# Seven block products for the Down projection of a pair in an attention and mixture-of-experts block

## The chip, the cores and the metric

The kernel runs on one core of a Trainium2 chip. The metric is the device time of one execution in microseconds. All arithmetic that matters here is fp32.

## The reference

One layer over 4096 tokens of 256 features. The input is normalised to `xn`, and three terms are added: the input, a windowed attention block with its own dense MLP, and a mixture of eight experts of which each token uses two.

```
xn = layernorm(x)
out = x + attn_block(xn) + experts(xn)

attn_block: q, k, v = xn@Wq+bq, ...;  window 64, 8 heads, softmax over a band
            y = layernorm(xn + o@Wo + bo)*gamma + beta
            y + gelu(y@W1 + b1)@W2 + b2           # 256 -> 1024 -> 256
experts:    top 2 of 8 by softmax(xn@gate_w.T + gate_b), shares made to sum to 1
            for each expert e (hidden size 816):
              h = silu((xn@gp_w[e].T + gp_b[e]) * (xn@up_w[e].T + up_b[e]))
              acc += share[:, e] * (h @ down_w[e].T + down_b[e])
```

## The kernel before

Tokens are sorted by expert into units. A unit is a pair of tiles (256 tokens) or a single tile (128 tokens) of one expert. 34 units are always worked through, in the list `UNITS`: 30 pairs, and singles at places 3, 7, 11 and 15. Five more at the end (`MAYBE`) run under a condition, by the function `whole`.

A unit needs three things: the gathered rows turned into `xT` (`gather`, `turned`), the hidden chunks, and Down. The hidden size 816 is 6 chunks of 128 (`FCM`) and a rest of 48 (`REM`). `glu` computes one chunk: gate and up matmuls into one PSUM bank `gu`, ScalarE adds the gate's bias (`gs`, L853), VectorE multiplies into `hT` (L854). The rest of a pair lies in one more chunk of `hT`: tile 0's on partitions 0 to 47, tile 1's on 64 to 111. `silu` runs on `hT` in place. Down (`results_rest` L896, `results` L907) takes the hidden tile as the stationary operand and the expert's weights `wd`, 256 columns wide, as the moving one, into one bank per tile (`pe`); `summed` (L917) adds the bias, which `wd` carries on all partitions, into `y`, and a DMA stores `y` to the table `done`. An fp32 matmul leaves two records in the trace.

The loop runs over steps b = 0 to 33. Step b computes the hidden chunks of unit b and the Down of unit b - 1. In the first 32 steps (`STEPS`) it also does one half (four heads, `hq` = b % 2) of the attention of two query tiles:

- `scores`: PE writes four banks `ps` (L960); VectorE adds the mask and takes the maximum into `pr` (L974); `exps` on ScalarE (L989)
- `merge`, four times, on GpSimd: two operations on `pr` (L1001, L1002). `apart`, on GpSimd: differences of neighbouring values into `xd` (L1009)
- `scale`, on VectorE: the reciprocal `rec` (L1019), then `pr` times `rec` (L1021), the sums of the second half (L1022, L1023), and on GpSimd `xd` times these (L1025)
- `flip`: PE transposes `pr` into a bank `pT` (L1030), VectorE masks it twice into `prT` (L1034). `flip_rest`: PE's two small transposes of `xd` into `pX` (L1043)
- `weigh`, `outputs`, and in each even step from the second on `closing` for the two tiles before (L1074, L1077, and their moments)

The order on every engine is written out by hand: `tc.manual_schedule` keeps the order of the code. Within a step it is: gathers, scores, `apart`, Down of the rest, chunk 0, chunk 1, `closing`, `scale`, Down, the load of `wd`, `turned`, projections for later tiles (steps 1 to 16), chunk 2, `flip`, chunk 3, `flip`, `flip_rest`, chunk 4, the rest, chunk 5, `weigh`. In steps 32 and 33 there is no attention and Down follows chunk 0. Behind the loop comes the Down of unit 33. The PSUM pool has seven banks; a new tile takes the one whose last use stands earliest in the order.

Behind the units the second part runs: the dense MLP. There `second` (L1198) already computes its product with W2 by seven block products in place of eight, with sums made by `sums_of_weights` and `sums_of_hidden`.

Of the kernel before, what the change touches and what calls it, by code (L numbers as in the profile page):

```python
# [32 lines left out]
F32 = mybir.dt.float32  # L33
# [8 lines left out]
P = 128  # L42
S = 4096
D = 256
# [10 lines left out]

REM = FE % P
REM_UP = P // 2
FM = FE - REM  # L60
FCM = FM // P
NT = S // P
G = 512
NG = S // G
# [24 lines left out]

GW, UW, RW, BW = 0, DC * FM, 2 * DC * FM, 2 * DC * FM + DC * P  # L90
GU = BW + 2 * FCM + 1
DN = FCE * D + D
HQ = 4
AHEAD = 4
WARM = 50
# [6 lines left out]
def block_kernel(ctx: ExitStack, tc: tile.TileContext, a: dict, out: bass.AP):  # L102
# [116 lines left out]

    att = ctx.enter_context(ExitStack())  # L220
    wqkv = pool(att, "wqkv", right)
    mask = wqkv.tile([P, 4, 2 * P], F32, tag="mask", name="mask")

# [87 lines left out]
    def make_mask():  # L311

        nc.gpsimd.memset(mask, 0.0)
        for kind in range(4):

            def keep(base, step, channel, m=mask[:, kind, :]):
                nc.gpsimd.affine_select(
                    out=m,  # L320
                    in_=m,
                    compare_op=ALU.is_ge,
                    fill=MASKED,
                    base=base,
                    pattern=[[step, 2 * P]],
                    channel_multiplier=channel,
                )

            keep(0, 1, -1)
            keep(2 * WIN, -1, 1)  # L330
            if kind == 0:
                keep(-WIN, 1, 0)
            if kind == 3:
# [551 lines left out]
    def silu(hT, lo, hi, on=slice(0, P)):  # L885
        nc.scalar.activation(hT[on, lo:hi, :], hT[on, lo:hi, :], AF.Silu)  # L886

    def silu_rest(hT):

        silu(hT, FCM, FCE, slice(0, REM_UP + REM if hT.shape[2] > P else REM))  # L890

    def results_rest(pds, w, hT):
        for t, pd in enumerate(pds):

            half = slice(t * REM_UP, (t + 1) * REM_UP) if len(pds) > 1 else slice(0, P)
            nc.tensor.matmul(  # L896
                pd,
                hT[half, FCM, t * P : (t + 1) * P],
                w[half, FCM * D : FCE * D],
                start=True,  # L900
                stop=False,
            )
# [9 lines left out]
                    stop=(f == FCM - 1),  # L912
                )

    def summed(y, pds, w):
        for t, pd in enumerate(pds):
            nc.vector.tensor_tensor(y[:, t, :], pd, w[:, FCE * D :], ALU.add)  # L917

    def down_rest(b, w, hT):

# [1 line left out]
        results_rest(pds, w, hT)  # L922
        return pds

    def down(b, pds, w, hT):
        at, n, _ = UNITS[b]
        results(pds, w, hT)
        y = he.tile([P, TB, D], F32, tag="y", name=f"y{b}")[:, 0:n, :]
        summed(y, pds, w)
        nc.sync.dma_start(out=rows(done, at, n), in_=y)  # L930

    def whole(b, w, wd, xT, hT, banks, gss, y):

        _, n, _ = UNITS[b]
        n_in = n * P
        for k, f in enumerate([FCM] + list(range(FCM))):
            pb = halves(banks[k % 3])[:, :, 0:n_in]
            gs = gss[k % 3][:, 0:n_in]
            if f == FCM:
                rest_of(w, xT, hT, pb, gs)  # L940
            else:
# [8 lines left out]
        summed(y, pds, wd)  # L950

    def scores(i, hq):

        g = i // TG
        ps = [halves(bank(f"ps{i}_{hq}_{hh}")) for hh in range(HQ)]
        for j in range(2):
            lo = (i + j) % TG * P
            for hh in range(HQ):
                r = slice(hh * DH, (hh + 1) * DH)
                nc.tensor.matmul(  # L960
                    ps[hh][:, j, :],
                    qts[g][r, hq, lo : lo + P],
                    kts[g][r, hq, lo : lo + 2 * P],
                    start=True,
                    stop=True,
                )
        kind = 0 if i == 0 else 2 if i == NT - 2 else 1
        pr = sp.tile([P, HQ, 2, 2 * P], F32, tag="pr", name=f"pr{i}_{hq}", bufs=1)

        nm = sp.tile([P, 2, HQ], F32, tag="nm", name=f"nm{i}_{hq}")  # L970
        sums = sp.tile([P, 2, HQ], F32, tag="sums", name=f"sums{i}_{hq}")
        for hh in range(HQ):
            for j in range(2):
                nc.vector.tensor_tensor_reduce(  # L974
                    out=pr[:, hh, j, :],
                    in0=ps[hh][:, j, :],
                    in1=mask[:, kind + j, :],
                    scale=-1.0,
                    scalar=-LOWEST,
                    op0=ALU.add,  # L980
                    op1=ALU.min,
                    accum_out=nm[:, j, hh : hh + 1],
                )
        return pr, nm, sums
# [26 lines left out]
            )  # L1011
        return xd

    def scale(i, hq, pr, sums, xd):

        rec = sp.tile([P, 2, HQ], F32, tag="rec", name=f"rec{i}_{hq}")
        same = sp.tile([P, 2, HQ], F32, tag="same", name=f"same{i}_{hq}")
        by_head = "p j h -> p h j"
        nc.vector.reciprocal(rec, sums)  # L1019
        first = pr[:, :, :, 0:P]  # L1020
        nc.vector.tensor_tensor(first, first, bcast(rec.rearrange(by_head), P, 3), ALU.mult)  # L1021
        nc.vector.tensor_reduce(same.rearrange(by_head), pr[:, :, :, P:], AX.X, ALU.add)  # L1022
        nc.vector.tensor_tensor(same, same, rec, ALU.mult)  # L1023
        xh = xd.rearrange("p j (h d) -> p j h d", h=HQ)
        nc.gpsimd.tensor_tensor(xh, xh, bcast(same, DH, 3), ALU.mult)  # L1025

    def flip(i, hq, j, pr):
        pb = bank(f"pT{i}_{hq}_{j}")
        for hh in range(HQ):
            nc.tensor.transpose(pb[:, hh * P : (hh + 1) * P], pr[:, hh, j, 0:P], ident)  # L1030

        prT = [sp.tile([P, HQ, P], F32, tag="prT", name=f"prT{i}_{hq}_{j}"), pr[:, :, j, P:]]
        for t, m in zip(prT, (first_keys, second_keys)):
            nc.vector.tensor_tensor(  # L1034
                t, pb.rearrange("p (h q) -> p h q", h=HQ), bcast(m, HQ, 1), ALU.mult
            )
        return prT
# [204 lines left out]
    hTs = [he.tile([P, FCE, B], F32, tag=f"hT{k}", name=f"hT{k}", bufs=1) for k in range(2)]  # L1242
    for k in range(2):
        nc.gpsimd.memset(hTs[k][:, FCM, :], 0.0)
    res = {0: residual(0)}
    xT = {}
    pos, oTs = {}, {}
# [11 lines left out]
    for b in range(ALWAYS):  # L1259
# [5 lines left out]
        def chunk(f):  # L1265
            glu(b, f, gus[b], xT[b], hT)

        if b + 2 < ALWAYS:
            xs[b + 2] = gather(b + 2)
        if attends:  # L1270
            pr, nm, sums = scores(i, hq)
            xd = apart(i, hq)
        if 0 < b < STEPS:
            pds = down_rest(b - 1, downs[b - 1], hTs[(b - 1) % 2])
        if b == 0:
            xT[0] = turned(0, xs.pop(0))
        if attends:
            exps(pr, nm, sums, 0, 3)
            merge(pr, 0)
        chunk(0)  # L1280
        if b >= STEPS:
            pds = down_rest(b - 1, downs[b - 1], hTs[(b - 1) % 2])
            down(b - 1, pds, downs.pop(b - 1), hTs[(b - 1) % 2])
        if attends:
            exps(pr, nm, sums, 3, 6)
            merge(pr, 1)
# [5 lines left out]
        if hq == 0 and i - 2 in res:  # L1292
            closing(i - 2, oTs.pop(i - 2), res.pop(i - 2))
            if i < STEPS:
                res[i] = residual(i)
        if attends:
            scale(i, hq, pr, sums, xd)
        if b == STEPS:
            att.close()
            wf = pool(ctx, "wf", right)  # L1300
# [14 lines left out]
        if b == STEPS + 1:  # L1315
# [2 lines left out]
            nc.vector.scalar_tensor_tensor(shift2, mv2[:, :, 0], -1.0, r2, ALU.mult, ALU.mult)  # L1318
            nc.vector.tensor_tensor(beta_b2, beta, b2, ALU.add)
            x2s[0] = second_loads(0)  # L1320
        if 0 < b < STEPS:
            down(b - 1, pds, downs.pop(b - 1), hTs[(b - 1) % 2])
        if b == ALWAYS - 1:
            load_unit(ALWAYS + 1)
        if b + 1 < ALWAYS:
# [28 lines left out]
        if attends:  # L1354

            if b == 0:
                prT0 = flip(i, hq, 0, pr)
                chunk(4)
            prT1 = flip(i, hq, 1, pr)
            added = flip_rest(i, hq, xd)  # L1360
        if b:
            chunk(4)
        n = b - (ALWAYS - len(MAYBE))
        if n >= 0:
            flags[ALWAYS + n] = nc.values_load(used[0:1, n : n + 1], min_val=0, max_val=1)
# [18 lines left out]
    down(ALWAYS - 1, pds, downs.pop(ALWAYS - 1), last)  # L1384
    load_unit(ALWAYS + 2)
    for b in range(ALWAYS, BLOCKS):
        at, n, _ = UNITS[b]
# [139 lines left out]
```

## Time and profile before

| | |
|---|---|
| runs | 1085.88, 1086.16, 1087.51 us, median 1086.16 |
| profiled execution | 1082.57 us, span 1080.4 us |
| TensorE clock granted | 1.00 |
| busy: TensorE, VectorE, ScalarE, GpSimd | 1069.1, 657.6, 526.9, 452.0 us |
| the loop's 32 attention steps | 82 to 797 us, about 22 us each |
| conditional units | 822 to 859 us |
| the dense MLP | 859 us to the end |

Busy time of the engines, in tenths, stands in the page in 40 slices. A line of a group has the source line, the engine, the operation, what is written and read, its shape, how often it ran, the busy time, the mean duration of one in ns, and the idle time ahead of it with what ended that. A line of a timeline has the start from the beginning of the span, the duration, the engine, the operation, and in brackets the idle time before it and what ended it.

### The profile page before, as it was taken

The numbers are of one execution on the slowest core, as the hardware profiler recorded it, in microseconds if no ns is written. First come the engines' busy times: TensorE is split into PE (matmuls) and PEld (weight loads), VectorE is DVE, ScalarE is ACT, GpSimd is POOL, SyncE is SP. The second block draws the span as 40 slices with busy tenths as digits, with TensorE's granted clock in tenths as the row PEclk, the third lists the DMA queues.
The fourth block names the chain that finished last, engine by engine and source line by source line (L and its number), as shares of the span: only waits on it lengthen the run. The fifth ranks groups of instructions, "written<-read, shape, count | busy, mean of one in ns | idle before, by whom it ended". The sixth has DMA issues, their size and how long they took to land. (4 is left out here: it accounts for less than half of the span.)

```text
span 1080.4 us, 19051 instructions
## 1 busy us (share of the span) xinstructions
PE 1069.1 (99%) x6802; PEld 857.4 (79%) x6802; DVE 657.6 (61%) x1709; ACT 526.9 (49%) x1225; POOL 452.0 (42%) x599
## 2 busy tenths in 40 slices
PE   9999999999999999999999999999999999999998
PEld 6577888887888788888888888888888847777778
DVE  6666666657666566666666766666533355555546
ACT  4527446554556545745564566555424363333320
POOL 5525544455445454554445534544520043222220
PEclk9999999999999999999999999999999999999999
DMA  8252445544445354544544545445575443333121
GB/s 274 84 221 92 142 137 177 177 151 154 160 142 187 132 164 159 202 142 159 171 180 142 181 149 199 142 139 184 177 242 223 160 141 111 97 96 97 59 64 40
DMA packets 61040, 163.42 MB, mean 151 GB/s; under 512 B 6576, under 2 KB 46896, under 8 KB 51472
## 3 DMA queue, kind: packets, MB, share of 16 engines
q1 hardware_dynamic: 53216, 143.92, 38.0%
q0 software_dynamic: 6480, 17.70, 6.2%
q8 instruction: 55, 0.90, 0.3%
q10 hardware_dynamic: 1248, 0.56, 0.2%
q14 instruction: 41, 0.34, 0.1%
HBM read 140.28 MB, written 21.89 MB: 150 GB/s over the span
## 5 line engine op out<-in xcount | busy, mean ns | idle before, releaser
L845 PE MATMUL gu<-xsT,wg 128*128 128x256 f32 (+1 forms) x1632 | 362.5, 369 | 0.7 <-ACT xsT L837 0.7
L845 PEld LDWEIGHTS gu<-xsT,wg 128*128 128x128 f32 x1632 | 289.1, 190 | 45.3 <-DVE nm L974 8.6
L853 ACT ACTIVATE gs<-gu,wg 128x256 f32<-128x256 f32 (+1 forms) x204 | 92.6, 454 | 255.8 <-PE gu L845 244.1
L854 DVE SCALAR_TENSOR_TENSOR hT<-gu,wg,gs 128x256 f32<-128x256 f32 (+1 forms) x204 | 95.0, 467 | 174.7 <-ACT gs L853 174.5
L1001 POOL TENSOR_TENSOR pr<-pr 128x256 f32<-128x256 f32 x128 | 93.2, 728 | 250.6 <-ACT pr L989 250.6
L907 PE MATMUL pe<-wd,hT 128*128 128x256 f32 x768 | 171.6, 379 | 0.0
L907 PEld LDWEIGHTS pe<-wd,hT 128*128 128x128 f32 x768 | 145.4, 190 | 20.5 <-issue 1.0
L1172 POOL DMA_INDIRECT got<-done,slot x64 | 64.4, 1007 | 176.6 <-DVE acc L1185 110.7
L1002 POOL TENSOR_TENSOR pr<-pr,ident 128x256 f32<-128x256 f32 x128 | 125.4, 979 | 10.0
L989 ACT ACTIVATE pr<-pr,nm 128x256 f32<-128x256 f32 x256 | 126.7, 497 | 0.4
L1127 PE MATMUL ph<-x2T,W 128*128 128x512 f32 x256 | 111.4, 593 | 1.1 <-ACT x2T L1117 1.1
L974 DVE CUSTOM_DVE_ANT_0 pr<-ps,mask 128x256 f32<-128x256 f32 x256 | 90.7, 420 | 22.8 <-PE ps L960 22.8
L1134 ACT ACTIVATE hf<-ph,b 128x512 f32<-128x512 f32 x64 | 43.4, 688 | 118.4 <-issue 54.6
L886 ACT ACTIVATE hT<-hT 128x512 f32<-128x512 f32 (+3 forms) x148 | 80.9, 546 | 32.0 <-DVE hT L854 22.4
L1127 PEld LDWEIGHTS ph<-x2T,W 128*128 128x128 f32 x256 | 48.0, 190 | 58.9 <-issue 53.6
L819 POOL DMA_INDIRECT xs<-xnd,token x71 | 68.8, 969 | 48.6 <-DVE paired_tiles L786 31.3
L1021 DVE TENSOR_TENSOR pr<-pr,rec 128x1024 f32<-128x1024 f32 x32 | 39.6, 1236 | 27.9 <-POOL pr L1001 27.9
L1208 DVE TENSOR_TENSOR acc<-u,acc 128x256 f32<-128x256 f32 x32 | 12.9, 422 | 70.2 <-ACT u L1211 69.6
L989 ACT ACT_TABLE_LOAD x31 | 39.8, 1283 | 23.7 <-DVE nm L974 23.6
L1022 DVE TENSOR_REDUCE same<-pr 128x8 f32<-128x1024 f32 x32 | 39.1, 1221 | 19.2 <-POOL pr L1002 19.2
L989 ACT ACTIVATION_READ_ACCUMULATOR pr<-pr,nm 128x1 f32 x256 | 48.3, 189 | 0.0
L1198 PE MATMUL s<-V,hv 128*128 128x128 f32 x384 | 44.2, 275 | 0.0
(231 smaller groups left out, 1573.3 us busy)
## 6 DMA issues: line engine op xcount, KB each, us to landing
wg<-in_gate_up SPq DMA_DIRECT2D x37, 1670.5 KB, 7.0
wd<-in_down SPq DMA_DIRECT2D x37, 1024.0 KB, 5.5
done<-y SPq DMA_DIRECT2D x30, 256.0 KB, 2.2
x<-in_x SPq DMA_DIRECT2D x8, 512.0 KB, 5.5
xnd<-xn SPq DMA_DIRECT2D x8, 512.0 KB, 4.3
res<-xnd SPq DMA_DIRECT2D x16, 256.0 KB, 2.9
x1d<-res SPq DMA_DIRECT2D x16, 256.0 KB, 2.2
x<-x1d SPq DMA_DIRECT2D x8, 512.0 KB, 4.7
```

The source lines that it names most:

```text
L819: nc.gpsimd.indirect_dma_start(out=x[:, t, :], out_offset=None, in_=xnd, in_offset=bass.IndirectOffsetOnAxis(ap=token[:, i : i + 1], axis=0),)
L845: nc.tensor.matmul(pb[:, k, :], w[:, lo : lo + P], xT[:, c, :], start=(c == 0), stop=(c == DC - 1),)
L853: nc.scalar.activation(gs, pb[:, 0, :], AF.Identity, bias=w[:, gb : gb + 1])
L854: nc.vector.scalar_tensor_tensor(hT[:, f, :], pb[:, 1, :], w[:, ub : ub + 1], gs, ALU.add, ALU.mult)
L886: nc.scalar.activation(hT[on, lo:hi, :], hT[on, lo:hi, :], AF.Silu)
L907: nc.tensor.matmul(pd, hT[:, f, t * P : (t + 1) * P], w[:, f * D : (f + 1) * D], start=False, stop=(f == FCM - 1),)
L974: nc.vector.tensor_tensor_reduce(out=pr[:, hh, j, :], in0=ps[hh][:, j, :], in1=mask[:, kind + j, :], scale=-1.0, scalar=-LOWEST, op0=ALU.a ...
L989: nc.scalar.activation(pr[:, hh, j, :], pr[:, hh, j, :], AF.Exp, bias=nm[:, j, hh : hh + 1], scale=-1.0, accum_out=sums[:, j, hh : hh + 1],)
L1001: nc.gpsimd.tensor_tensor(first, first, second, ALU.add)
L1002: nc.gpsimd.tensor_tensor(second, second, bcast(ident, 2, 1), ALU.mult)
L1127: nc.tensor.matmul(ph, W1[:, c, f * P : (f + 1) * P], x2T[:, c, :], start=(c == 0), stop=(c == DC - 1),)
L1172: nc.gpsimd.indirect_dma_start(out=y, out_offset=None, in_=done, in_offset=bass.IndirectOffsetOnAxis(ap=slot[:, k, i : i + 1], axis=0),)
```

## The change

Down of a pair is computed by seven products of blocks. The hidden tile pair is cut into four blocks: by tile, and by even and odd chunks; the weights likewise by even and odd chunks and by halves of their columns. Each product is three matmuls of 128x128 by 128x128. The four products that more than one output block needs, or that start such a sum, go first and into a shared bank `sh`; the other three go into the banks `pe` behind the rest's product.

Four differences of weights (`sums_of_down`) are made on GpSimd, behind `apart` and ahead of the merges; one of them overwrites a block of `wd`. Three sums of the hidden blocks (`sums_of_experts_hidden`) are made on VectorE, between the scores and chunk 0; a fourth inside `results_of_pair`. ScalarE copies the shared bank into `y`, VectorE makes three additions on it, then `rec` and the scaling of `pr` follow, and then the two additions of the banks `pe`. The rest of `scale` is now `scale_rest`. Down stands ahead of `scale`, not behind it.

The bias no longer lies on all partitions of `wd`: the rest's weights carry it in one more row, and `hT` holds ones there, set once ahead of the loop. So `silu_rest` runs once for each tile, and `wd` is 256 columns narrower. `flip_rest` comes behind chunk 4. `prT` is written into `pr`, and the mask has three kinds in place of four.

```diff
-DN = FCE * D + D
+DN = FCE * D
...
     def silu_rest(hT):
-        silu(hT, FCM, FCE, slice(0, REM_UP + REM if hT.shape[2] > P else REM))
+        for t in range(hT.shape[2] // P):
+            silu(hT[:, :, t * P : (t + 1) * P], FCM, FCE, slice(t * REM_UP, t * REM_UP + REM))
...
+    def sums_of_down(b, w):
+        ts = he.tile([P, 3, FCH, P], F32, tag="ts", name=f"ts{b}", bufs=1)
+        t2, t3, t4 = (ts[:, k] for k in range(3))
+        m = blocks_of_weights(w)
+        b11, b12, b21, b22 = m[:, 0, 0], m[:, 0, 1], m[:, 1, 0], m[:, 1, 1]
+        t1 = b12
+        for out_, left_, right_ in ((t3, b22, b12), (t1, b12, b11), (t2, b22, t1), (t4, b21, t2)):
+            nc.gpsimd.tensor_tensor(out_, left_, right_, ALU.subtract)
+        return ts
+
+    def sums_of_experts_hidden(b, hT):
+        ss = he.tile([P, 2, FCH, P], F32, tag="ss", name=f"ss{b}", bufs=1)
+        s1, s2 = (ss[:, k] for k in range(2))
+        m = blocks_of_hidden(hT)
+        a11, a12, a21, a22 = m[:, 0, 0], m[:, 0, 1], m[:, 1, 0], m[:, 1, 1]
+        nc.vector.tensor_tensor(s1, a21, a22, ALU.add)
+        nc.vector.tensor_tensor(s2, s1, a11, ALU.subtract)
+        nc.vector.tensor_tensor(a21, a11, a21, ALU.subtract)
+        return ss
+
+    def results_of_pair(b, pds, w, hT, ss, ts):
+        n, m = blocks_of_hidden(hT), blocks_of_weights(w)
+        c1, c2 = slice(0, P), slice(P, D)
...
+        shared = bank(f"sh{b}").rearrange("p (k n) -> p k n", n=P)
+        product(shared[:, 0], n[:, 0, 0], m[:, 0, 0], True)
+        nc.vector.tensor_tensor(n[:, 0, 0], n[:, 0, 1], ss[:, 1], ALU.subtract)
+        product(shared[:, 1], ss[:, 1], ts[:, 0], True)
+        product(shared[:, 2], n[:, 1, 0], ts[:, 1], True)
+        product(shared[:, 3], ss[:, 0], m[:, 0, 1], True)
+        product(pds[0][:, c1], n[:, 0, 1], m[:, 1, 0], stop=False)
+        product(pds[1][:, c1], n[:, 1, 1], ts[:, 2])
+        product(pds[0][:, c2], n[:, 0, 0], m[:, 1, 1])
+        return shared
+
+    def summed_of_pair(y, pds, shared):
+        q = y.rearrange("p t (h n) -> p (t h) n", n=P)
+        nc.scalar.copy(q, shared)
+        nc.vector.tensor_tensor(q[:, 1], q[:, 0], q[:, 1], ALU.add)
+        nc.vector.tensor_tensor(q[:, 2], q[:, 1], q[:, 2], ALU.add)
+        both = q.rearrange("p (t h) n -> p h t n", h=2)
+        nc.vector.tensor_tensor(both[:, 1], q[:, 1:3], bcast(q[:, 3], 2, 1), ALU.add)
+        yield
         for t, pd in enumerate(pds):
-            nc.vector.tensor_tensor(y[:, t, :], pd, w[:, FCE * D :], ALU.add)
+            nc.vector.tensor_tensor(y[:, t, :], pd, y[:, t, :], ALU.add)
...
-        prT = [sp.tile([P, HQ, P], F32, tag="prT", name=f"prT{i}_{hq}_{j}"), pr[:, :, j, P:]]
+        prT = [pr[:, :, j, k * P : (k + 1) * P] for k in range(2)]
...
     for k in range(2):
         nc.gpsimd.memset(hTs[k][:, FCM, :], 0.0)
+        for behind in (REM, REM_UP + REM):
+            nc.gpsimd.tensor_tensor(
+                hTs[k][:, FCM, :],
+                hTs[k][:, FCM, :],
+                ident[:, behind : behind + 1].to_broadcast([P, B]),
+                ALU.add,
+            )
...
         if attends:
             pr, nm, sums = scores(i, hq)
             xd = apart(i, hq)
+        ts = sums_of_down(b - 1, downs[b - 1]) if b and UNITS[b - 1][1] > 1 else None
...
             merge(pr, 0)
+        ss = sums_of_experts_hidden(b - 1, before) if ts else None
         chunk(0)
...
+        made = iter(())
+        if 0 < b < STEPS:
+            made = down(b - 1, pds, downs.pop(b - 1), before, (ss, ts))
+            next(made)
         if attends:
-            scale(i, hq, pr, sums, xd)
+            rec = scale(i, hq, pr, sums)
+            list(made)
+            scale_rest(i, hq, pr, rec, xd)
...
-        if 0 < b < STEPS:
-            down(b - 1, pds, downs.pop(b - 1), hTs[(b - 1) % 2])
...
             prT1 = flip(i, hq, 1, pr)
-            added = flip_rest(i, hq, xd)
         if b:
             chunk(4)
+        if attends:
+            added = flip_rest(i, hq, xd)
```

More of the change, by code (lines that the diff above doesn't have):

```diff
@@ L61 @@
 FCM = FM // P
+FCH = FCM // 2
 NT = S // P
@@ L221, in block_kernel @@
     wqkv = pool(att, "wqkv", right)
-    mask = wqkv.tile([P, 4, 2 * P], F32, tag="mask", name="mask")
+    mask = wqkv.tile([P, 3, 2 * P], F32, tag="mask", name="mask")
     first_keys = wqkv.tile([P, P], F32, tag="first_keys", name="first_keys")
@@ L315, in make_mask @@
         nc.gpsimd.memset(mask, 0.0)
-        for kind in range(4):
+        for kind in range(3):
             def keep(base, step, channel, m=mask[:, kind, :]):
@@ L332, in make_mask @@
                 keep(-WIN, 1, 0)
-            if kind == 3:
+            if kind == 2:
                 keep(2 * P - WIN - 1, -1, 0)
@@ L888, in silu_rest @@
     def silu_rest(hT):
-        silu(hT, FCM, FCE, slice(0, REM_UP + REM if hT.shape[2] > P else REM))
+        for t in range(hT.shape[2] // P):
+            silu(hT[:, :, t * P : (t + 1) * P], FCM, FCE, slice(t * REM_UP, t * REM_UP + REM))
     def results_rest(pds, w, hT):
         for t, pd in enumerate(pds):
-            half = slice(t * REM_UP, (t + 1) * REM_UP) if len(pds) > 1 else slice(0, P)
+            half = slice(t * REM_UP, (t + 1) * REM_UP)
             nc.tensor.matmul(
@@ L913, in results, with blocks_of_weights, blocks_of_hidden @@
                 )
-    def summed(y, pds, w):
+    def blocks_of_weights(w):
+        return w[:, 0 : FCM * D].rearrange("p (m e h n) -> p e h m n", e=2, h=2, n=P)
+    def blocks_of_hidden(hT):
+        return hT[:, 0:FCM, :].rearrange("p (m e) (t n) -> p t e m n", e=2, n=P)
+    def sums_of_down(b, w):
[7 more added lines that the diff above has]
+        return ts
@@ new lines, in sums_of_experts_hidden, with product @@
+    def sums_of_experts_hidden(b, hT):
[10 more added lines that the diff above has]
+        c1, c2 = slice(0, P), slice(P, D)
+        def product(to, left, right, start=False, stop=True):
+            for f in range(FCH):
+                nc.tensor.matmul(
+                    to,
+                    left[:, f, :],
+                    right[:, f, :],
+                    start=(start and f == 0),
+                    stop=(stop and f == FCH - 1),
+                )
[9 more added lines that the diff above has]
+        return shared
@@ L919, in down_rest, with summed @@
+    def summed(y, pds):
+        for t, pd in enumerate(pds):
+            nc.vector.tensor_copy(y[:, t, :], pd)
     def down_rest(b, w, hT):
@@ L923, in down_rest, with down @@
         return pds
-    def down(b, pds, w, hT):
+    def down(b, pds, w, hT, sums):
         at, n, _ = UNITS[b]
-        results(pds, w, hT)
         y = he.tile([P, TB, D], F32, tag="y", name=f"y{b}")[:, 0:n, :]
-        summed(y, pds, w)
+        if n > 1:
+            shared = results_of_pair(b, pds, w, hT, *sums)
+            yield from summed_of_pair(y, pds, shared)
+        else:
+            results(pds, w, hT)
+            yield
+            summed(y, pds)
         nc.sync.dma_start(out=rows(done, at, n), in_=y)
@@ L949, in whole @@
         results(pds, wd, hT)
-        summed(y, pds, wd)
+        summed(y, pds)
     def scores(i, hq):
@@ L966, in scores @@
                 )
-        kind = 0 if i == 0 else 2 if i == NT - 2 else 1
+        kinds = 0 if i == 0 else 1, 2 if i == NT - 2 else 1
         pr = sp.tile([P, HQ, 2, 2 * P], F32, tag="pr", name=f"pr{i}_{hq}", bufs=1)
@@ L976, in scores @@
                     in0=ps[hh][:, j, :],
-                    in1=mask[:, kind + j, :],
+                    in1=mask[:, kinds[j], :],
                     scale=-1.0,
@@ L1012, in apart, with scale, scale_rest @@
         return xd
-    def scale(i, hq, pr, sums, xd):
+    def scale(i, hq, pr, sums):
         rec = sp.tile([P, 2, HQ], F32, tag="rec", name=f"rec{i}_{hq}")
-        same = sp.tile([P, 2, HQ], F32, tag="same", name=f"same{i}_{hq}")
-        by_head = "p j h -> p h j"
         nc.vector.reciprocal(rec, sums)
         first = pr[:, :, :, 0:P]
-        nc.vector.tensor_tensor(first, first, bcast(rec.rearrange(by_head), P, 3), ALU.mult)
-        nc.vector.tensor_reduce(same.rearrange(by_head), pr[:, :, :, P:], AX.X, ALU.add)
+        nc.vector.tensor_tensor(
+            first, first, bcast(rec.rearrange("p j h -> p h j"), P, 3), ALU.mult
+        )
+        return rec
+    def scale_rest(i, hq, pr, rec, xd):
+        same = sp.tile([P, 2, HQ], F32, tag="same", name=f"same{i}_{hq}")
+        nc.vector.tensor_reduce(
+            same.rearrange("p j h -> p h j"), pr[:, :, :, P:], AX.X, ALU.add
+        )
         nc.vector.tensor_tensor(same, same, rec, ALU.mult)
@@ L1244, in block_kernel @@
         nc.gpsimd.memset(hTs[k][:, FCM, :], 0.0)
+        for behind in (REM, REM_UP + REM):
[4 more added lines that the diff above has]
+                ALU.add,
+            )
     res = {0: residual(0)}
@@ L1269, in block_kernel @@
             xs[b + 2] = gather(b + 2)
+        before = hTs[(b - 1) % 2][:, :, 0 : UNITS[b - 1][1] * P]
         if attends:
@@ L1272, in block_kernel @@
             xd = apart(i, hq)
+        ts = sums_of_down(b - 1, downs[b - 1]) if b and UNITS[b - 1][1] > 1 else None
         if 0 < b < STEPS:
-            pds = down_rest(b - 1, downs[b - 1], hTs[(b - 1) % 2])
+            pds = down_rest(b - 1, downs[b - 1], before)
         if b == 0:
@@ L1279, in block_kernel @@
             merge(pr, 0)
+        ss = sums_of_experts_hidden(b - 1, before) if ts else None
         chunk(0)
         if b >= STEPS:
-            pds = down_rest(b - 1, downs[b - 1], hTs[(b - 1) % 2])
-            down(b - 1, pds, downs.pop(b - 1), hTs[(b - 1) % 2])
+            pds = down_rest(b - 1, downs[b - 1], before)
+            list(down(b - 1, pds, downs.pop(b - 1), before, (ss, ts)))
         if attends:
@@ L1320, in block_kernel @@
             x2s[0] = second_loads(0)
-        if 0 < b < STEPS:
-            down(b - 1, pds, downs.pop(b - 1), hTs[(b - 1) % 2])
         if b == ALWAYS - 1:
@@ L1383, in block_kernel @@
     pds = down_rest(ALWAYS - 1, downs[ALWAYS - 1], last)
-    down(ALWAYS - 1, pds, downs.pop(ALWAYS - 1), last)
+    sums = None
+    if UNITS[ALWAYS - 1][1] > 1:
+        sums = (
+            sums_of_experts_hidden(ALWAYS - 1, last),
+            sums_of_down(ALWAYS - 1, downs[ALWAYS - 1]),
+        )
+    list(down(ALWAYS - 1, pds, downs.pop(ALWAYS - 1), last, sums))
     load_unit(ALWAYS + 2)
@@ L1459, in rows, with rest @@
         return m.reshape(E, -1, P, n).transpose(0, 2, 1, 3).reshape(E, P, -1)
-    def rest(up, gate):
+    def rest(up, gate, behind=0.0):
         m = np.zeros((E, P, up.shape[-1]), np.float32)
@@ L1465, in rest @@
         m[:, REM_UP : REM_UP + REM] = up[:, FM:]
+        m[:, REM] = m[:, REM_UP + REM] = behind
         return m
@@ L1484 @@
             rows(down[:, :FM], D),
-            rest(down, down),
-            np.broadcast_to(v["down_b"][:, None, :], (E, P, D)),
+            rest(down, down, v["down_b"]),
         ],
```

## The prediction

> **What bounds the kernel now.** I read the page first, then TensorE's timeline for the steps of the unit loop, then the groups by shape, the chain of waits, and the timelines of VectorE (DVE) and GpSimd (POOL) for the same step.
>
> ```profile
> span 1080.4 us, 19051 instructions
> PE 1069.1 (99%) x6802; PEld 857.4 (79%) x6802; DVE 657.6 (61%) x1709; ACT 526.9 (49%) x1225; POOL 452.0 (42%) x599
> ```
>
> A busy PE proves little, since matmul ends are modelled; the starts prove it. In steps 17 and 19, 21, ... 29 every group starts at the same offset to 0.01 us, and steps last 20.86 (odd) or 22.58 us (even): PE waits for nobody. This is step 17, which starts at 451.90 (all offsets "+" below count from a step's start):
>
> ```profile
> 457.17 5.34 PE L907 MATMUL pe<-wd,hT 128*128 128x256 f32 x24
> 462.35 0.60 PE L832 MATMUL pts<-ident,xs 128*128 128x128 f32 x4
> ...
> 464.52 0.60 PE L1030 MATMUL pT<-ident,pr 128*128 128x128 f32 x4
> ```
>
> The Down of a pair takes 462.35 - 457.17 = 5.18 us for 24 records (an fp32 matmul leaves two), 0.216 each. The seven-product form already exists for W2, in the chain that ended last:
>
> ```profile
> 889.95 12.51 PE s L1198 x112
> ```
>
> 112 records of 128 columns: 0.1117 us each. The cover, in the same step 17, first POOL, then DVE:
>
> ```profile
> 456.04 0.73 POOL L1001 TENSOR_TENSOR pr<-pr 128x256 f32<-128x256 f32 x1 [8.21 <-ACT pr L989]
> ...
> 460.52 0.73 POOL L1001 TENSOR_TENSOR pr<-pr 128x256 f32<-128x256 f32 x1
> 461.33 1.76 POOL L1002 TENSOR_TENSOR pr<-pr,ident 128x256 f32<-128x256 f32 x1
> 464.62 0.62 POOL L1025 TENSOR_TENSOR xd<-xd,same 128x256 f32<-128x256 f32 x1 [1.53 <-DVE same L1023]
> ```
> ```profile
> 455.83 0.08 DVE L974 DVE_READ_ACCUMULATOR2_ANT nm<- 128x1 f32 x1
> 456.85 0.48 DVE L854 SCALAR_TENSOR_TENSOR hT<-gu,wg,gs 128x256 f32<-128x256 f32 x1 [0.94 <-ACT gs L853]
> ...
> 461.28 1.23 DVE L1021 TENSOR_TENSOR pr<-pr,rec 128x1024 f32<-128x1024 f32 x1 [1.41 <-POOL pr L1001]
> ```
>
> See three things. POOL idles 8.21 us before its merges: room. L1021 ends at +10.61 and PE's pT wants it at +12.62: 2 us of slack, no more. And L1002, else 0.73 us, takes 1.76 beside L1021. The same from the other side, early in the kernel:
>
> ```profile
> 15.17 0.56 POOL L467 TENSOR_SCALAR xn<-x,r_a,shift 128x256 f32<-128x256 f32 x1
> 15.29 0.45 DVE L185 SCALAR_TENSOR_TENSOR t_a<-mv,t_a 128x4 f32<-128x4 f32 x1
> ```
>
> L185 takes 0.16 us undisturbed (its median); here it ends when POOL's instruction ends. At 17.95 (0.47, beside 17.85 to 18.41) it does so again. So a DVE operation with two SBUF operands and a POOL operation exclude each other, whole instruction by whole instruction; what waits ends soon after: L185 0.01 us after POOL's end, L1002 0.58 after L1021's. L854 and the scores, with one tensor in SBUF and one in PSUM, keep their times beside merges.
>
> **The change, part by part.**
>
> *Matmuls.* 7 products x 3 x 2 = 42 records x 0.1117 = 4.69 us for 5.18: -0.49 a pair, 30 pairs in the unit loop and just behind it, -14.7 us. The late units keep the plain form. Here a rule speaks against the change: the Trainium skill, "TensorE: Matmul & The Clock Gate", Part 3 (packing small matmuls), says that a weight load overlaps running matmuls only when its row group differs. All rows are in use here, and one load takes 0.19 us: unhidden, 42 x (0.19 + 0.11) = 12.6 us against 24 x (0.19 + 0.22) = 9.8, so +2.8 a pair, +84 us. The row of 112 records with full-height loads in 12.51 us denies it; I take the row.
>
> *Weight differences (POOL).* Four subtractions of 128x384. Between L1009 (128 elements, 459 ns) and L1067 (512, 1272 ns) lies 1.00 us each, 4.0 a pair. In POOL's order they stand behind the next unit's gathers and `apart`, before the merges. In step 17 that is: L1025 to about +15, two gathers to 17.5, `apart` (behind pX, now one chunk later, at 17) to 18.4, the four to 22.5, which is +1.8 of step 18. Its merges start at +4.1: hidden, by the 8 us of idle time.
>
> *Hidden sums (DVE).* From L1158 (1024 elements, 1216 ns) and L1023 (8, 176 ns): 0.56 us for 384 elements, 0.30 for 128, 0.43 for 256. s1, s2, a11-a21 stand behind the scores (+4.01), before chunk 0's product; a12-s2 behind chunk 1; the three additions of banks before `rec`. All have two SBUF operands, as POOL's merges do, so they take turns with the merges (M1 to M8). For step 17, by the handoffs above (a waiting 384-element addition ends 0.41 after POOL's end, 256 0.28, 128 0.14; a waiting merge 0.58 after DVE's end): s1 ends +4.57, M1 5.15, s2 5.56, M2 6.14, third sum 6.55, M3 7.13, M4 7.94, a12-s2 8.35, M5 8.93; ScalarE's copy of the shared bank ends +8.75, first addition 9.07, M6 9.7, second 9.84, M7 10.4, third 10.7, M8 11.3 (rec passes meanwhile), L1021 11.3 to 12.4.
>
> GpSimd's page ("GPSIMD Engine Reference", 8. Key points) names contention with such DVE instructions, but no size. By counting busy time alone, DVE's 3.3 us more would vanish in its idle time (232 of 365 us busy from 432 to 797, so 7 to 8 us a step are free), and the sum would be rival 1's; by the turn-taking of the rows they don't.
>
> *What PE then meets.*
> - Short odd steps (17, 19, ... 31; 8): pT now wants L1021 at 12.62 - 0.49 = +12.13; it comes at about 12.4, and the scores start 0.1 or so late: stall 0.35, net -0.14 each, -1.1.
> - Short even steps (18 to 30; 7): `closing` occupies DVE to +9.2, the shared bank is copied by +10.5; then the additions take turns with M8 and with L1067 (1.27 us, its load lands at about +11.3): L1021 ends about +14.4, pT wants it at 14.34 - 0.49 = 13.85. Stall 0.55, net +0.06, +0.4.
> - Steps with projections (1, 5, 9, 13 and 2, 6, 10, 14; 8): 1.7 us more of PE work ahead of pT covers it. -0.49 each, -3.9.
> - Steps of a single unit (3, 7, 11, 15; 4): chunks 0 and 1 take half as long, so the products start at +3.60, the second needs s2 at +4.27 and gets it at 5.6, the third needs 6.6: stall 1.6, net +1.1, +4.5. (Cover gone: chunk work.)
> - Steps 4, 8, 12, 16 have a single's Down: 0. Steps 32 and 33: no merges, -0.5 each, -1.0.
> - Behind the loop: the three sums wait for the last SiLU; the old order met that chunk last, the new one in the first product. Stall 0.5 + 0.9, net +0.9.
> - Step 0: the ones for the bias row are four more POOL additions (0.62 to 0.73 each) ahead of its first merges, where PE already waits 0.48 us for L1021. About 2.7 us, half of it in idle time before the merges: +1.3.
>
> Sum: -1.1 + 0.4 - 3.9 + 4.5 - 1.0 + 0.9 + 1.3 = +1.1 us.
>
> *The rest at nothing, between -1 and +1 together.* pX one chunk later: takes the later L1025 off PE's path and makes `apart` later, inside POOL's idle time. SiLU of the remainder in two pieces: 2 x 0.31 for 0.42, ScalarE half idle. The bank additions behind L1021 (same count) delay xsT, which the next step reads. On SP the `done` store waits for them, at +13 as before, with the next `wd` load behind it, needed a step later. One bank more per pair: by the built order gu2 takes the bank of chunk 0, released early. Masks and weights get smaller: nothing waits for them.
>
> The profiled execution took 1082.57 us, 2.2 more than its span; the median of the runs, 1086.16, is 3.59 above it. 1082.57 + 1.1 + 3.59 = 1087.3.
>
> **Rivals.**
> 1. *The turns cost nothing* (faster). If additions of 384 elements slip in beside merges, L1021 ends near +11.1 or 12.8, no short step stalls, a single step stalls 0.9 (+0.4): 23 x -0.49 + 1.6 - 1.0 + 0.9 + 1.3 = -8.5: 1077.7. For it: no row shows this size side by side. Against: 1.76 and 0.45 above.
> 2. *Each turn costs its startup too* (slower). A merge takes 0.73 alone and 0.58 behind a wait; if 0.15 is paid at each of seven handoffs, L1021 comes 1.05 us later. The 15 short steps have no slack left, so 15.8 us, and 1.2 in the single steps: 1104; at half that price 1096. It decides from 0.07 us per step on, as the sum is then beyond 0.2%. Against: the measured ends behind a wait. For: one engine never had so many turns in a row here.
> 3. *The matmuls save nothing*: from 0.123 us per record on. In the neighbourhood of other shapes that isn't shown; 15 us more, 1102.
>
> **How the numbers follow.** 0.2% (2.2 us) is about what a measurement of this kernel can tell from no change. Forecast case, 0.47: own range 1083 to 1092, as a handoff won by the other engine moves L1021 by 0.3 us in 15 steps; of it 0.07 lies below 1084.0, 0.27 within 0.2%, 0.13 above 1088.3. Rival 1: 0.20; rival 2: 0.30; rival 3: 0.03. So faster 0.27, same 0.27, slower 0.46. The range 1077 to 1100 leaves out some of rival 1 below and the dear part of rival 2 above.
>
> **What would show it.** Down's group: 42 records in 4.69 us where no wait falls in. s2 and the third sum reported longer than 0.56 (with their wait), merges up to 1.2. PE waiting for L1021 at pT by 0.3 to 0.6 us in short steps and for s2 by 1.3 in steps 3, 7, 11, 15, and none in 1, 5, 9, 13. Wrong if sums last 0.56 with merges beside them (rival 1), or if L1021 ends beyond +13 in step 17 (rival 2).

## The result, and the profile after

The changed kernel took 1095.89 us (median of 4 runs, 1093.34 to 1098.24), the kernel before beside it 1086.02 (1084.92 to 1087.51): ratio 1.0095, interval 1.0081 to 1.0109, so it is 0.95% slower. The forecast was 1087.3 within 1077 to 1100. The profiled execution took 1093.34 us, 10.77 more than that of before; its span is 11.1 longer.

The page of the changed kernel, its first lines:

```profile
span 1091.5 us, 20566 instructions
...
PE 1063.0 (97%) x7342; PEld 860.5 (79%) x7342; DVE 806.6 (74%) x1919; ACT 547.9 (50%) x1286; POOL 576.7 (53%) x721
```

TensorE is busy 6 us less although the span is 11 longer: it now waits. Its timeline in step 17, which starts at 455.19:

```profile
460.45 0.83 PE L960 MATMUL sh<-wd,hT 128*128 128x128 f32 x6
...
464.50 0.83 PE L960 MATMUL pe<-wd,hT 128*128 128x128 f32 x6
465.17 0.60 PE L834 MATMUL pts<-ident,xs 128*128 128x128 f32 x4
...
467.70 0.63 PE L1118 MATMUL pT<-ident,pr 128*128 128x128 f32 x4 [0.20 <-DVE pr L1100]
```

The seven products take 465.17 - 460.45 = 4.72 us, as forecast (4.69; before 5.18). Then pT, wanted at +12.15, starts at +12.51. The reason is in the timelines of POOL and VectorE (DVE) for the same step:

```profile
459.33 0.92 POOL L1082 TENSOR_TENSOR pr<-pr 128x256 f32<-128x256 f32 x1 [2.46 <-ACT pr L1070]
460.33 0.92 POOL L1083 TENSOR_TENSOR pr<-pr,ident 128x256 f32<-128x256 f32 x1
461.21 1.04 POOL L1082 TENSOR_TENSOR pr<-pr 128x256 f32<-128x256 f32 x1
...
465.69 0.79 POOL L1083 TENSOR_TENSOR pr<-pr,ident 128x256 f32<-128x256 f32 x1
```
```profile
459.11 0.55 DVE L946 TENSOR_TENSOR ss<-hT 128x384 f32<-128x384 f32 x1
459.70 0.97 DVE L947 TENSOR_TENSOR ss<-ss,hT 128x384 f32<-128x384 f32 x1
460.59 1.08 DVE L948 TENSOR_TENSOR hT<-hT 128x384 f32<-128x384 f32 x1
...
466.11 1.45 DVE L1100 TENSOR_TENSOR pr<-pr,rec 128x1024 f32<-128x1024 f32 x1
```

Read the ends in turn. DVE's first sum ends at 459.66, POOL's first merge at 460.25 (0.59 later), the second sum at 460.67 (0.42 later), the second merge at 461.25 (0.58), the third sum at 461.67 (0.42). The wait shows as part of the instruction: a sum of this size takes 0.55 us alone and 0.97 to 1.08 beside a merge. The last merge ends at +11.29 (forecast 11.3) and the scaling L1100 at +12.37 (forecast 12.4).

By steps, from the starts of the scores' matmuls in both profiles, and from there on from the same groups of matmuls (the 32 attention steps of the kernel before end at 776.83, where step 32 begins):

| part | forecast, us | measured, us |
|---|---|---|
| step 0 | +1.3 | +0.8 |
| step 1 | -0.5 | +0.2 |
| steps 2, 6, 10, 14 and 5, 9, 13 | -3.4 | -3.3 |
| steps 3, 7, 11, 15 | +4.5 | +4.8 |
| steps 4, 8, 12, 16 | 0 | +0.8 |
| 8 short odd steps | -1.1 | -0.6 |
| 7 short even steps | +0.4 | +2.4 |
| steps 32 and 33 | -1.0 | +4.1 |
| pair behind the loop | +0.9 | +1.0 |
| late units | 0 | +0.9 |
| sum | +1.1 | +11.1 |

In the row of steps 32 and 33, step 32 gives +2.2 and step 33 +1.9. All of the loop except the even steps came within 0.8 us a row. Of the 10.0 us between the two sums, 5.1 lie in steps 32 and 33 and 2.0 in the short even steps.

*A short even step.* Step 18 starts at 475.97; POOL, then DVE, then TensorE:

```profile
487.36 1.40 POOL L1155 TENSOR_TENSOR res<-res,bo 128x512 f32<-128x512 f32 x1 [0.20 <-DMA res<-xnd]
```
```profile
487.67 1.38 DVE L986 TENSOR_TENSOR y<-y 128x256 f32<-128x256 f32 x1
488.97 0.19 DVE L1098 RECIPROCAL rec<-sums 128x8 f32<-128x8 f32 x1
489.26 1.23 DVE L1100 TENSOR_TENSOR pr<-pr,rec 128x1024 f32<-128x1024 f32 x1
```
```profile
490.63 0.63 PE L1118 MATMUL pT<-ident,pr 128*128 128x128 f32 x4 [0.65 <-ACT gs L855]
```

The load of `res` lands just as DVE stands between two additions of banks. POOL's addition to it takes the turn, and L986, 0.42 us alone, takes 1.38. L1100 ends at 490.49, 0.14 before pT starts; the row names ScalarE, but pT at +14.66 in place of +13.85 is L1100's lateness.

*A step of a single unit.* Step 15 (414.24), TensorE: the work of chunks 0 and 1, which covers the sums, is half as long, and the second product waits for s2 (the second sum, L947) as forecast (1.19; 1.3 was said).

```profile
417.83 0.83 PE L960 MATMUL sh<-wd,hT 128*128 128x128 f32 x6
419.86 0.91 PE L960 MATMUL sh<-ts,ss 128*128 128x128 f32 x6 [1.19 <-DVE ss L947]
```

*Step 32.* It has no merges, yet DVE and ScalarE stand still. DVE, then ScalarE:

```profile
784.81 0.42 DVE L1149 TENSOR_TENSOR oT<-po,added 128x256 f32<-128x256 f32 x1 [2.73 <-PE gu L847]
...
790.56 0.56 DVE L970 TENSOR_TENSOR hT<-hT,ss 128x384 f32<-128x384 f32 x1 [1.86 <-remote]
```
```profile
787.71 0.47 ACT L855 ACTIVATE gs<-gu,wg 128x256 f32<-128x256 f32 x1 [4.96 <-remote]
790.74 0.59 ACT L981 COPY y<-sh 128x512 f32<-128x512 f32 x1 [2.55 <-remote]
```

(`remote` stands where no releaser was found.) All four wait for the semaphore of TensorE, whose groups stand much earlier in its timeline: `po` from 780.93, `gu` from 781.94. The updates of that semaphore in the trace are late: at 784.79, 787.64 and 790.50. In the kernel before, with `gu` from 776.83, the first two follow at once; DVE, then ScalarE:

```profile
776.96 0.42 DVE L1061 TENSOR_TENSOR oT<-po,added 128x256 f32<-128x256 f32 x1
```
```profile
778.91 0.47 ACT L853 ACTIVATE gs<-gu,wg 128x256 f32<-128x256 f32 x1 [1.27 <-PE gu L845]
```

*Step 33.* POOL now has the differences of unit 33's weights beside VectorE's small operations for the second norm, which stand ahead of the copies of `xT`. POOL, then DVE, then TensorE:

```profile
816.91 1.05 POOL L937 TENSOR_TENSOR wd<-wd 128x384 f32<-128x384 f32 x1
818.04 1.04 POOL L937 TENSOR_TENSOR ts<-wd 128x384 f32<-128x384 f32 x1
```
```profile
817.14 0.86 DVE L189 TENSOR_SCALAR t_b<-t_b 128x32 f32<-128x32 f32 x1
818.03 0.19 DVE L192 TENSOR_TENSOR r_b<-y_b,t_b 128x32 f32<-128x32 f32 x1
818.26 0.87 DVE L1422 SCALAR_TENSOR_TENSOR shift<-mv,r_b 128x32 f32<-128x32 f32 x1
```
```profile
819.85 1.13 PE L847 MATMUL gu<-xsT,wg 128*128 128x256 f32 x4 [1.22 <-DVE xsT L839]
```

L189 begins at 817.14 and ends at 818.00, just after POOL's 817.96; L1422 ends at 819.13 after POOL's 819.08. Each of these two operations on 32 columns lasts until a POOL instruction of 384 columns is done. In the kernel before, L189's counterpart had nothing beside it:

```profile
809.04 0.18 DVE L187 TENSOR_SCALAR t_b<-t_b 128x32 f32<-128x32 f32 x1
```

L189 has one tensor operand only. So the operations that take turns with POOL are more than those with two operands in SBUF, which the prediction named. Not every operation with one does: the reciprocal of 32 columns (L182), in the middle of POOL's first difference, keeps its 0.35 us.

### The profile page after: what moved, and what is told of

Same layout as the page of the kernel before. It is cut to its first block, busy times and chain, and to the rows that moved or that the text cites. A ratio compares the mean times of both kernels' runs of the same rounds, so it can differ in the third digit from the quotient of the medians.

```text
span 1091.5 us, 20566 instructions
## 1 busy us (share of the span) xinstructions
PE 1063.0 (97%) x7342; PEld 860.5 (79%) x7342; DVE 806.6 (74%) x1919; ACT 547.9 (50%) x1286; POOL 576.7 (53%) x721
## 5 line engine op out<-in xcount | busy, mean ns | idle before, releaser
L1082 POOL TENSOR_TENSOR pr<-pr 128x256 f32<-128x256 f32 x128 | 114.9, 898 | 85.4 <-ACT pr L1070 85.4
L856 DVE SCALAR_TENSOR_TENSOR hT<-gu,wg,gs 128x256 f32<-128x256 f32 (+1 forms) x204 | 91.6, 460 | 63.8 <-ACT gs L855 63.7
L1083 POOL TENSOR_TENSOR pr<-pr,ident 128x256 f32<-128x256 f32 x128 | 106.0, 828 | 10.0
L888 ACT ACTIVATE hT<-hT 128x512 f32<-128x512 f32 (+2 forms) x179 | 83.9, 484 | 27.2 <-DVE hT L856 22.4
L1113 POOL TENSOR_TENSOR xd<-xd,same 128x256 f32<-128x256 f32 x32 | 19.7, 617 | 93.9 <-DVE same L1111 93.8
L937 POOL TENSOR_TENSOR ts<-wd 128x384 f32<-128x384 f32 x60 | 60.2, 1003 | 4.4 <-issue 2.1
L960 PE MATMUL pe<-wd,hT 128*128 128x128 f32 x360 | 50.1, 275 | 0.2 <-DVE hT L970 0.2
L1100 DVE TENSOR_TENSOR pr<-pr,rec 128x1024 f32<-128x1024 f32 x32 | 44.3, 1386 | 5.6 <-POOL pr L1082 2.8
L1118 PE MATMUL pT<-ident,pr 128*128 128x128 f32 x256 | 38.9, 274 | 7.2 <-DVE pr L1100 4.0
```

Of the source, the lines that this page charges most:

```text
L856: nc.vector.scalar_tensor_tensor(hT[:, f, :], pb[:, 1, :], w[:, ub : ub + 1], gs, ALU.add, ALU.mult)
L1082: nc.gpsimd.tensor_tensor(first, first, second, ALU.add)
L1083: nc.gpsimd.tensor_tensor(second, second, bcast(ident, 2, 1), ALU.mult)
```

## The experiments

**All other parts, without the seven products.**

```diff
-        if n > 1:
+        if sums:          # sums is None for every unit: plain Down
             shared = results_of_pair(b, pds, w, hT, *sums)
```

> Changed kernel with the plain Down for every pair (12 matmuls of 256 columns each as before; no differences of weights, no sums of hidden blocks, no additions of banks). The other parts stay: bias in the weights' rest rows with the ones in hT, SiLU of the remainder in two pieces, transposes of xd one chunk later, prT in place, smaller mask. Theory T (turn-taking of the new two-SBUF-operand additions with POOL): step lengths return to those of before, but for step 0 (+0.8) and the four steps with a single's Down (+0.2 each), and the last steps and the tail return too: +1.6 us against before, 1087.6. Rival O (the other parts cost the time): 1091 to 1095, with step 32 still waiting about 2.7 us for its VectorE work.

Measured: 1085.78 against 1083.84, ratio 1.0019 (1.0012 to 1.0025). Step 0 is 17.97 (before 17.22), steps 4, 8, 12 23.42 (23.22), step 16 20.88 (20.69), all others within 0.02 of before, and step 32 is again without a wait. The late units start their next stage 36.6 us after their first matmul, 35.8 before. So the other parts cost 0.8 + 0.8 + 0.8 us, and T holds. (The late units' share was not forecast.)

**The products on raw blocks.**

```diff
-        for out_, left_, right_ in ((t3, b22, b12), (t1, b12, b11), (t2, b22, t1), (t4, b21, t2)):
-            nc.gpsimd.tensor_tensor(out_, left_, right_, ALU.subtract)
-        return ts
+        return m[:, 1, 1], m[:, 1, 1], m[:, 1, 0]
...
-        nc.vector.tensor_tensor(s1, a21, a22, ALU.add)       # and s2, a11-a21, a12-s2
+        return m[:, 1, 0], m[:, 1, 0]
```

> Changed kernel with the seven products on raw blocks: neither the four differences of weights on POOL nor the four sums of hidden blocks on VectorE are computed (the pairs' results are so not those of the reference); the three additions of banks stay. T: the products save 0.49 us in each of 30 pairs, nothing meets a wait in single or odd steps, 0 to 0.2 us may stay in seven even steps: before - 14.7 + 1.6 + 0 to 1.4, so 1073 to 1074.5. Rival M (products save nothing beside other shapes): 1087 or more.

Measured: ratio 0.9939 (0.9926 to 0.9953), -6.3 us. The products do save (step 5: 22.09, step 2: 23.60), so M is out. But T's figure (about 12 us below before) is missed too. Odd short steps are 20.62 to 20.64 in place of 20.37: the three additions of banks alone hold up the scaling. Steps 3, 7, 11, 15 are 19.14 in place of 18.37, longer than before (18.87): TensorE's weight loads for `po` wait there twice, 0.40 and 0.44 us, for VectorE's copies of prT. VectorE is next to bound these steps once the sums are gone.

**One half of the sums at a time.** First without the differences of weights, then without the sums of hidden blocks (each edit is one half of the diff above).

> Changed kernel without the four differences of weights on POOL (products use raw weight blocks, so results of pairs are not the reference's); sums of hidden blocks and additions of banks stay. T: they lie in POOL's idle time in the loop, so steps 2 to 31 keep their lengths (20.79 / 22.94 / 20.07); gone are the 0.65 us of step 1 and most of the late part's loss (steps 32, 33 and behind, about 5 us): 1090 to 1091. Rival P (POOL's added 4 us a step are what makes the merges late): short steps lose their waits, 1080.

> Changed kernel without the four sums of hidden blocks on VectorE (products use raw hidden blocks, so results of pairs are not the reference's); differences of weights and additions of banks stay. T: single steps fall from 20.07 to 18.37, odd short steps from 20.79 to 20.37, even short steps from 22.94 to between 22.1 and 22.6: -6.8 - 3.4 - 2 to -6 us, and about -1 behind the loop: 1079 to 1083. Rival B (the additions of banks, which stand right before the scaling, make it late): single steps fall alike, short steps keep their time: 1088.

Measured without the differences: ratio 1.0067 (1.0053 to 1.0080), +7.1. Most steps keep their lengths (odd 20.78 to 20.80, single 20.07, even 22.90 to 23.06, but 22.09 in steps 20 and 30), so the differences were hidden in the loop, as forecast. In steps 20 and 30 of this run POOL's addition to `res` came later, at +12.56 and +13.11 in place of +11.2 to +11.4, and so fell behind the additions of banks. Step 1 keeps its 22.78 too, against T. Step 32 lost its wait and 2.7 us. Most of that went again: 0.6 us in step 33 and 1.7 behind the loop, where TensorE ran 3.41 us at half its clock (last section). In step 33 the sums of hidden blocks met POOL's subtractions for W2; POOL, then DVE:

```profile
801.96 1.27 POOL L1234 TENSOR_TENSOR V<-W 128x512 f32<-128x512 f32 x1 [17.48 <-SPq L1345]
803.30 1.46 POOL L1234 TENSOR_TENSOR V<-W,V 128x512 f32<-128x512 f32 x1
804.72 1.58 POOL L1234 TENSOR_TENSOR V<-W 128x512 f32<-128x512 f32 x1
```
```profile
801.97 1.67 DVE L940 TENSOR_TENSOR ss<-hT 128x384 f32<-128x384 f32 x1 [0.70 <-ACT hT L888]
803.67 1.50 DVE L941 TENSOR_TENSOR ss<-ss,hT 128x384 f32<-128x384 f32 x1
805.09 1.62 DVE L942 TENSOR_TENSOR hT<-hT 128x384 f32<-128x384 f32 x1
```

It is the plainest view of the turns: the ends are 803.23 (POOL), 803.64 (DVE), 804.76, 805.17, 806.30, 806.71. TensorE waited 1.82 and 0.60 us there.

Without the sums of hidden blocks: ratio 0.9945 (0.9932 to 0.9959), -5.5. Single steps 19.13 to 19.16 (T had said 18.37, and missed as with raw blocks), odd short 20.62, even 22.19 to 22.23 (22.5 in two), step 1 22.09. So the hidden sums cost 0.93, 0.17, 0.74 and 0.69 us there. The other 0.25 of each odd step (20.62 against 20.37) are then left to the additions of banks: T and B each name a part. With both halves out or the hidden sums alone out, the time is the same within 0.1%: the differences on POOL are nearly free in the loop.

**Is it the turns, or VectorE's added work?** The merges are left out, and VectorE does all it did.

```diff
-        nc.gpsimd.tensor_tensor(first, first, second, ALU.add)
-        nc.gpsimd.tensor_tensor(second, second, bcast(ident, 2, 1), ALU.mult)
+        pass
```

> Changed kernel without POOL's merges of the scores (the eight operations of 128x256 a step; the attention is so not that of the reference); all additions of Down stay on VectorE. T (what costs is the turn-taking with the merges, not VectorE's own work): s2 and the third sum last 0.55 as s1 does; odd short steps 20.37, even ones 22.09, step 1 22.09, single steps about 19.2 to 19.3 (s2 comes at +5.15 and is wanted at +4.27); the late part as in the changed kernel. Sum against the changed kernel -13, about 3 below before. Rival D (VectorE's added 150 us of work are late by themselves): steps as in the changed kernel, at most 3 us below it. Step 32 is a second look at its waits without a releaser: if they are part of this order of work, it lasts again 2.2 longer than before.

Measured: ratio 0.9970 (0.9958 to 0.9982), -2.8. Odd short steps 20.37, step 1 22.09, single steps 19.39, even ones 22.09 to 22.47. The loop is 13.2 us shorter than in the changed kernel; 1.6 of that lie in step 0, which has no Down. The late part did not stay as it was, against T: step 32 had no wait and was 2.7 us shorter, step 33 was 3.5 longer, with TensorE at half its clock for 3.41 us there. By shape, the groups of the changed kernel and then of this one:

```profile
L948 DVE TENSOR_TENSOR hT<-hT 128x384 f32<-128x384 f32 x30 | 31.9, 1062 | 0.0
...
L947 DVE TENSOR_TENSOR ss<-ss,hT 128x384 f32<-128x384 f32 x30 | 27.8, 925 | 1.0
```
```profile
L947 DVE TENSOR_TENSOR ss<-ss,hT 128x384 f32<-128x384 f32 x30 | 17.7, 589 | 1.0
...
L948 DVE TENSOR_TENSOR hT<-hT 128x384 f32<-128x384 f32 x30 | 17.6, 587 | 0.0
```

The mean of a sum falls from 925 and 1062 ns to 589 and 587. VectorE has the same instructions in both, so rival D is out: what costs in the loop is the turns. Leaving out the merges also frees POOL and lets the scaling begin earlier, so the 13 us are an upper bound of what the turns cost; the fall of the sums is the turns alone.

**Where the turn falls.** Two edits, each of which moves a small piece of work.

```diff
         nc.scalar.copy(q, shared)
+        yield                      # the three additions of banks come behind the scaling
         nc.vector.tensor_tensor(q[:, 1], q[:, 0], q[:, 1], ALU.add)
...
-        yield
```

> Changed kernel with the three additions of banks behind the scaling of the scores instead of ahead of it; nothing else moves. T: the scaling starts when the last merge is done, some 0.5 to 1.4 us earlier: odd short steps 20.37, even ones 22.1 unless POOL's addition to the residual (1.27 us) now takes the turn right ahead of the scaling (then 22.5); single steps, step 1 and the late part stay. Sum against the changed kernel -3.4 -3 to -6. Rival: the sums of hidden blocks alone make the last merge late, and steps stay within 0.1 of the changed kernel's.

```diff
             scale_rest(i, hq, pr, rec, xd)
+            if hq == 0 and i > 0:
+                residual_rest(res[i])      # the POOL addition, taken out of residual()
```

> Changed kernel with POOL's addition of the bias to the residual (128x512, even steps only) put behind the product of xd on POOL; its load stays where it was. T: in even steps no addition of banks waits for it, the scaling starts 0.9 us earlier: even short steps 22.09 to 22.2 in place of 22.94, all others stay: -5.5 us against the changed kernel. Rival D (VectorE's own work): no change.

Measured, additions of banks behind the scaling: ratio 1.0015 (1.0007 to 1.0023). Odd short steps 20.40, even 22.09: the waits for the scaling are gone from the short steps, and the rival is out. Against T, the single steps grew from 20.07 to 20.44: the additions now stand ahead of the copies of prT on VectorE, and TensorE's weight loads for `po` wait up to 0.44 us for these copies.

Measured, residual later: ratio 1.0028 (1.0018 to 1.0039). All seven even steps are 22.09, all others unchanged to 0.02: the 0.85 us of a short even step were that one POOL operation in the wrong gap. It is the same loss as most of the 0.74 us in the run without hidden sums: there the additions of banks are done by +11.57, POOL's addition meets the scaling in their place, and the scaling ends at +13.8 to +14.1 and not at +14.5. The time fell by more than the forecast 5.5 us because step 32 had no wait here either, though the order of work there is the same.

**Only where it pays.**

```diff
+        blocks = 1 < b < STEPS and UNITS[b - 1][1] > 1 and UNITS[b][1] > 1
-        ts = sums_of_down(b - 1, downs[b - 1]) if b and UNITS[b - 1][1] > 1 else None
+        ts = sums_of_down(b - 1, downs[b - 1]) if blocks else None
...
-            half = slice(t * REM_UP, (t + 1) * REM_UP)
+            half = slice(t * REM_UP, (t + 1) * REM_UP) if len(pds) > 1 else slice(0, P)
...
-        nc.gpsimd.memset(hTs[k][:, FCM, :], 0.0)             # and two additions of 128x256
+        for t, behind in enumerate((REM, REM_UP + REM)):
+            one = ident[:, behind : behind + 1].to_broadcast([P, P])
+            nc.gpsimd.tensor_tensor(hTs[k][:, FCM, t * P : (t + 1) * P], one, one, ALU.mult)
```

The two moves above are in it as well.

> Seven products only in the 22 steps where both the unit and the one before it are pairs, from step 2 to 31; the plain Down in step 1, in the four steps of a single unit, in steps 32 and 33 and behind the loop. The additions of banks stand behind the scaling, the addition to the residual behind the product of xd, the ones for the bias row are written by two operations per buffer in place of three, and a single's remainder is again multiplied over all 128 rows. T: 23.6 in steps 2, 6, 10, 14, 22.09 in 5, 9, 13, 20.37 in odd and 22.09 in even short steps, all others as before: 22 x -0.49 = -10.8 us against before. Rival (the sums of hidden blocks still delay the scaling): odd 20.6, even 22.3: -7.

Measured: 1072.81 us against 1083.59, ratio 0.9897 (0.9883 to 0.9912): 10.8 us below before, as T said, and faster than both kernels. Steps: 20.40 and 22.09 in short ones, 22.13 and 23.60 in those with projections, 18.87 in single ones, 23.23 in 4, 8, 12. The rival is out. The turns are still there, as L947 and L948 take 966 and 1080 ns in the mean, but these 22 steps no longer wait for their ends by more than 0.04 us. TensorE in its step 17 meets no wait above that:

```profile
455.10 0.83 PE L960 MATMUL sh<-wd,hT 128*128 128x128 f32 x6
...
460.26 1.89 PE L847 MATMUL gu<-xsT,wg 128*128 128x256 f32 x8
461.99 0.60 PE L1118 MATMUL pT<-ident,pr 128*128 128x128 f32 x4
```

**Step 32 once more.**

> The changed kernel itself once more, with nothing edited, for step 32: there the changed kernel's profile has ScalarE waiting 4.96 us and VectorE 1.86 us with no releaser named, and the step lasts 2.66 us longer than in the changed kernel's relatives without these waits. If the order of work causes it, the profile shows it again (chunk 0 to chunk 1 of unit 32 in 10.0 us). If it is an accident of one execution or of the moment in which transfers land, the profile may be without it (7.35 us), and the time against before comes out up to 2.7 us lower than the first comparison's +9.9, near +7.3. Loop steps are expected as in the first profile: 20.79, 22.73 to 23.07, 20.07.

Measured: ratio 1.0109 (1.0091 to 1.0127). The wait is there again: TensorE's first three updates come 4.53, 6.03 and 8.97 us after the start of the loop's last `po` matmul, where the kernel with the later residual has them at 0.3, 2.2 and 3.5. So it is no accident of one execution. The loop's steps are those of the first profile to 0.2 us. Step 33 is 3.0 us longer than there, with longer waits and TensorE at half its clock for 3.41 us (last section). DMA traffic alone does not make the wait of step 32: over 5 us from about 1 us into that step the DMA engines are busy for a share of 0.97 in both profiles of the changed kernel, and of 0.96 with the later residual, which had no wait.

## Why the prediction was right and where it was not

The total fell inside the range and on the side given the most chance, but the time was 8.6 us above the forecast, and outside the 1083 to 1092 that the forecast case had for its own. It lies where rival 2 put it at half its price (1096), and rival 2 is refuted: that the range held is in part luck. In the loop the mechanism held; most of the difference comes from places it was not applied to, and 2.7 us from a wait in step 32 that it does not explain.

- *Matmuls* (-0.49 a pair): right. 42 records in 4.72 us; the steps with nothing in the way gave -0.49 (2, 6, 10, 14). The row of 112 records was the right one to take, and rival 3 is out.
- *Turn-taking*: right in the loop; in step 17 each end from s1 to L1021 came within 0.1 us of its forecast. Rival 1 is out (sums of 0.97 to 1.08 us beside merges). Rival 2 is out as well: handoffs cost what the rows of before said, no startup on top. Only the class of operations was too narrow (L189).
- *Short odd steps* (-0.14 each): -0.07 measured; the stall was 0.36, forecast 0.35, and pT itself took 0.03 longer.
- *Short even steps* (+0.06 each): +0.34 measured. The sum had one collision with the addition to the residual, at about the right place. It was mis-sized: pT's stall was 0.81 in place of 0.55.
- *Single steps* (+1.1 each): +1.2. The cause was right, but VectorE's copies of prT stood close behind: without the sums these steps fell to 19.14 only, where T had said 18.37.
- *Step 1* (-0.49): wrong, +0.20. It was counted among the covered steps, but its loss lies in the products, 0.65 us, not at pT; without the hidden sums or the merges it is gone.
- *Steps 32 and 33* (-1.0): wrong, and the largest miss. "No merges" was taken for "no turns". In step 33 POOL has the subtractions for W2 and the next differences, and both met VectorE: +1.9. Step 32 gained 0.5 where nothing waited (its relatives) and lost 2.7 to TensorE's late signals. They came in both profiles of the changed kernel and in none of its eight relatives, of which three (no merges, banks behind, residual later) have the same order of work there but reach step 32 between 5 and 13 us earlier. What delays the signals stays open; no run took it apart.
- *The rest at nothing*: the steps with a single's Down lost 0.2 each and the late units 0.9. The remainder's matmul over 64 rows took 0.63 us from its start to that of the next group, 0.53 over 128 rows, and the chunks behind it 0.10 more. With 128 rows again (last version), 23.23 and 20.69 are back.

## What to carry to other kernels

Count an added VectorE operation with two SBUF operands at its own time plus the rest of the POOL instruction it may meet (here 0.97 to 1.67 us for 0.55), and do this for every stage in which POOL works, not only for the one where the collision was first seen. Then look at the one instruction that TensorE waits for, and at what stands in the gap ahead of it: one move of three small additions cleared all 15 short steps here, another of one POOL operation the seven even ones. A saving that is paid only in steps with cover should be taken only there: with both moves, 22 of 30 pairs gave 10.8 us; without them, all 30 cost 10. No run has both moves and all 30 pairs.

## What was not expected of the hardware

TensorE's granted clock was halved for 3.41 us behind short waits of the late part, in four of the profiles (without differences, without merges, banks behind, and the second one of the changed kernel). In the last, TensorE waited 1.29 and 0.55 us in step 33, and the windows of that stretch show it (the width, busy time and count of TensorE, its weight loads, VectorE, ScalarE and GpSimd, then the granted clock, the DMA share and GB/s):

```profile
806.00:810.00 4.00, 2.42 (x17) 1.74 (x16) 3.89 (x3) 0.52 (x2) 3.92 (x4) 1.00 0.69 231
810.00:813.40 3.40, 3.14 (x14) 3.14 (x15) 1.75 (x3) 0.18 (x1) 1.33 (x1) 0.53 0.01 4
```

A product of six records then took up to 1.44 us, start to start, in place of 0.67. The Trainium skill, "TensorE: Matmul & The Clock Gate" (HAM oscillation), warns of idle gaps above about 3.4 us. No gap here was that long: waits of 0.3 to 1.8 us, two in a row, stood ahead of it, and not each time: behind the loop the waits of 0.45 and 0.79 us stood ahead of a halved clock with the banks behind, and of a full one in the changed kernel's first profile. So a wait in the late part can cost more than its length, by an estimate from the 3.41 us at half clock up to 1.7 us.

The times of single executions agree with this. Those of the changed kernel, of both measurements, took 1093.3 and 1094.1 us where the mean granted clock was 1.00, 1096.9 to 1098.2 at 0.998 and 0.997, and 1098.6 and 1100.5 at 0.995. All four of the version that takes the products only where they pay have 1.00. What decides whether the clock falls was not tested.
